# First attention, last six segments: the sum of the two gated terms moves from GpSimd into the turning on TensorE

## The chip, the cores and the metric

The kernel runs on one core of a Trainium2 chip. The metric is the device time of one launch in microseconds (us), lower is better. A profiled execution also has a span, from its first to its last recorded instruction. The engines are called TensorE (PE in the profile, its weight loads PEld), VectorE (DVE), ScalarE (ACT), GpSimd (POOL) and SyncE (SP).

## The reference, cut to what matters

The whole reference has two layers, each of an attention and a mixture of experts. The change lies in the first attention, which walks over segments of 64 tokens with a running memory `M` and normaliser `Z`:

```python
H, DK, DV, LSEG = (16, 64, 64, 64)          # B = 4 sequences of 512 tokens, D = 128
gate = sigmoid(betas)                        # one value per head and column v
def step(carry, seg):
    M, Z = carry
    q, k, v = ...                            # (B, H, 64, 64) each, of this segment
    scores = where(mask, -inf, q @ k.T / 8)
    att_dot = softmax(scores) @ v
    sq, sk = elu(q) + 1, elu(k) + 1
    att_mem = sq @ M / (sq @ Z.T)
    M_new, Z_new = M + sk.T @ v, Z + sk.sum(axis=-2)
    att = gate * att_mem + (1.0 - gate) * att_dot
    out = att.reshape(B, LSEG, H * DV) @ Wo
```

The sum in `att` is what the change is about: a gated memory term plus a gated softmax term, of which the product with `Wo` is then taken.

## The kernel before, in words

**Segments.** `attn0` walks over 32 segments `n` = 0 to 31, eight to a sequence. Each segment handles 64 tokens of 16 heads. A "segment" is one turn of the loop `for n in range(nseg)`; the order in which each engine gets its work is written out by hand there, and is kept (`pin`). The instructions of one segment are, in the order of the loop:

- `elu_exp(n + 1, 0)`: ScalarE, exp and relu of the next queries.
- `scores(n + 1)`: TensorE, 16 products `sc` (64x64), then VectorE the masked minimum `E` (line 686).
- `memory(n)`: TensorE, 16 products `mm`; VectorE a reciprocal `rm` (743) and the division `t` (744), which writes the tile `t1`; GpSimd multiplies it by the gate (763).
- `elu(n + 1, 0)`: VectorE, `elu` (709), which reads two tiles in SBUF.
- `turned(n - 2, n + 1)`: TensorE turns the finished attention of segment `n - 2` (eight transposes `tn<-ident,t`) and the elu keys of segment `n + 1` (eight transposes `tn<-ident,elu`), line 722, into one PSUM tile; ScalarE copies both out (`attT` in four pieces, `sk`).
- `update(n)`: TensorE, 16 products `mu`; VectorE adds them to the memory (`mz`, 778).
- `attend(n)`: TensorE, 16 products `dot`; VectorE a maximum and a reciprocal `rd` (797, 743), the division `t` (744, tile `t2`) and a maximum over sums (800); GpSimd multiplies by the other gate (801) and adds `t1` (802).
- `elu_exp(n + 2, 1)`, `scores_exp(n + 1)` on ScalarE, `elu(n + 2, 1)` on VectorE (709).

**Work between.** Up to segment 25 chunks of the q, k and v projections (`pp`, `pv`) stand in each segment as well; from segment 26 on there are none. Every fourth segment `output(h)` takes the 32 products `po` with `Wo`. In segment 31 and behind the loop the work of the next layer's experts (`ph`, `eo`) is mixed in, and `turned(30)`, `turned(31)` and `output(7)` come there.

**Buffers.** All of `sc`, `mm`, `tn`, `mu`, `dot`, `po`, `ph` take a tile of the same PSUM ring (`wide`), which has four buffers here: each takes the buffer of the fourth one before it, and waits until that one has been read. `t1` and `t2` have two buffers each, so segment `n` writes the tile of segment `n - 2`.

**Who waits for whom.** `mm` of segment `n` needs the memory that VectorE's `mz` of segment `n - 1` left. The turning of segment `n - 2` needs GpSimd's last write to `t2`.

Of the kernel before, what the change touches and what calls it, by code (L numbers as in the profile page):

```python
# [102 lines left out]
def bc(ap, axis, n):  # L103

    shape = list(ap.shape)
    return ap.unsqueeze(axis).to_broadcast(shape[:axis] + [n] + shape[axis:])


class Kernel:
# [257 lines left out]
    def wide(self, name):  # L367

        bufs = 4 if self.four else 3
        return self.banks.tile([P, 2, S], F32, name=name, tag="w", bufs=bufs)  # L370
# [228 lines left out]
    def attn0(self, xnT, g0, stack, between):  # L599
# [4 lines left out]
        nc, tc = self.nc, self.tc  # L604
        halves = [slice(0, 64), slice(64, 128)]
# [13 lines left out]
        for k in range(4):  # L619
            t = pool.tile([P, 4, 2, DK + 1], F32, name=f"vone{k}", bufs=1)  # L620
            nc.gpsimd.memset(t[:, :, :, DK : DK + 1], 1.0)
            vone.append(t)
        qkv, vd, attT, seg = {}, {}, {}, {}
# [45 lines left out]
        def blocks(n, w):  # L669
            s = n % 4  # L670
            return qkv[n // 4][w][:, s * 8 : s * 8 + 8, :]

        def scores(n):

            q, k = blocks(n, 0), blocks(n, 1)
            ps = wide(f"sc{n}")
            for hp in range(4):
                for p in range(2):
                    for a in range(2):
                        self.mm1(  # L680
                            ps[halves[a], p, hp * 64 : hp * 64 + 64],
                            lhsT=k[halves[p], 2 * hp + a, :], rhs=q[halves[p], 2 * hp + a, :],
                            start=True, stop=True,
                        )
            e = pool.tile([P, 2, 4, LSEG], F32, name=f"E{n}", tag="E")
            self.vec1(nc.vector.tensor_tensor(  # L686
                e, ps[:, :, 0:256].rearrange("p x (hp c) -> p x hp c", hp=4),
                bc(bc(self.cap, 1, 4), 1, 2), ALU.min,
            ))
            seg[n]["e"] = e  # L690
# [5 lines left out]
        def last(n):  # L696
            return n % 8 == 7
# [14 lines left out]
        def turned(att=None, own=None):  # L712

            ps = wide(f"tn{att}_{own}").rearrange("p x (w hp c) -> p x w hp c", w=2, hp=4)
            each = [(0, hp, x) for hp in range(4) for x in range(2) if att is not None]
            each += [(1, hp, x) for hp in range(4) for x in range(2) if own is not None]
            for w, hp, x in each:
                if w:
                    src = seg[own][1][halves[x], 2 * hp : 2 * hp + 2, :].rearrange("d a j -> d (a j)")
                else:  # L720
                    src = seg[att]["att"][halves[x], hp].rearrange("i p v -> i (p v)")
                self.pin(nc.tensor.transpose(ps[:, x, w, hp], src, self.ident[halves[x], halves[x]]))  # L722
            if att is not None:
                attended(att, ps[:, :, 0])
            if own is not None:
                t = seg[own]["sk"] = pool.tile([P, 4, 2, DK], F32, name=f"sk{own}", tag="sk")
                self.act1(t, ps[:, :, 1].rearrange("p x hp d -> p hp x d"), AF.Copy)

        def values(n):

            for p in range(2):
                src = vd[n // 4][p].rearrange("(s hp r) d -> s r hp d", s=4, hp=4)
                nc.sync.dma_start(out=vone[n % 4][:, :, p, 0:DK], in_=src[n % 4])

        def heads(ps):

            return ps[:, :, 0 : 4 * (DK + 1)].rearrange("p x (y v) -> p x y v", v=DK + 1)

        def over(t):
            return t.rearrange("p (x hp) y d -> p x (hp y) d", x=2)  # L740

        def divided(ps, t, r, sums):
            self.vec1(nc.vector.reciprocal(r, sums))
            self.vec1(nc.vector.tensor_tensor(t, heads(ps)[:, :, :, 0:DK], bc(r, 3, DK), ALU.mult))  # L744

        def memory(n):


            mz, sq = self.mz[(n % 8 + 1) % 2 + 1 if n % 8 else 0], seg[n][0]
            ps = wide(f"mm{n}")  # L750
            for hp in range(4):
                for p in range(2):
                    for a in range(2):
                        at = (2 * a + hp // 2) * (DK + 1)
                        self.mm1(
                            ps[halves[(a + hp) % 2], p, at : at + DK + 1],
                            lhsT=sq[halves[p], 2 * hp + a, :], rhs=mz[halves[p], hp, a, :],
                            start=True, stop=True,
                        )
            t = seg[n]["t1"] = pool.tile([P, 4, 2, DK], F32, name=f"t1{n}", tag="t1")  # L760
            r = pool.tile([P, 2, 4], F32, name=f"rm{n}", tag="rm")
            divided(ps, t.rearrange("p hp y d -> p y hp d"), r, heads(ps)[:, :, :, DK])
            nc.gpsimd.tensor_mul(t, t, self.gate)  # L763
# [16 lines left out]
        def attend(n):  # L780


            e, v = seg[n]["e"], vone[n % 4]
            ps = wide(f"dot{n}")
            for u in range(2):
                for p in range(2):
                    for hp in (2 * u, 2 * u + 1):
                        for a in range(2):
                            at = (2 * u + p) * (DK + 1)
                            self.mm1(  # L790
                                ps[halves[(a + hp) % 2], a, at : at + DK + 1],
                                lhsT=e[halves[a], p, hp, :], rhs=v[halves[a], hp, p, :],
                                start=True, stop=True,
                            )
            both = pool.tile([P, 2, 2, 4], F32, name=f"rd{n}", tag="rd")
            sums = both[:, 0]
            self.vec1(nc.vector.tensor_scalar_max(sums, heads(ps)[:, :, :, DK], SUM_MIN / 2))
            t = pool.tile([P, 4, 2, DK], F32, name=f"t2{n}", tag="t2")
            divided(ps, over(t), both[:, 1], sums)
            self.vec1(nc.vector.tensor_tensor(self.sums0, both, self.sums0, ALU.max))  # L800
            nc.gpsimd.tensor_mul(t, t, gate2)  # L801
            nc.gpsimd.tensor_add(t, t, seg[n]["t1"])  # L802
            seg[n]["att"] = t

        def attended(n, ps):

            if n % 4 == 0:

                attT[n // 4] = pool.tile([P, 16, 4, 32], F32, name=f"attT{n}", tag="attT")
            src = ps.rearrange("p h (a u) (t c) -> p c a u h t", a=2, c=16)  # L810
            dst = attT[n // 4][:, :, n % 4].rearrange("p c (u y t) -> p c u y t", u=2, y=4)
            for h in range(2):
                for a in range(2):
                    self.act1(dst[:, :, :, (a + h) % 2 * 2 + a], src[:, :, a, :, h], AF.Copy)
# [39 lines left out]
        for n in range(nseg):  # L854
            if n % 4 == 3:
                todo = project((n + 1) // 4 + 1)
            elif n == 0:
                todo = ahead
            each = 2 if n == 0 else 4 if n < 3 or n % 4 != 2 else 0
            nxt = n + 1 < nseg  # L860
            more = nxt and not last(n + 1)
            if n + 2 < nseg:
                values(n + 2)
            if nxt:
                elu_exp(n + 1, 0)
                scores(n + 1)
            memory(n)
            if nxt:
                elu(n + 1, 0)
            if n > 1 or more:  # L870
                turned(n - 2 if n > 1 else None, n + 1 if more else None)
            if not last(n):
                update(n)
            for f, *args in between.get(n - 0.5, []):
                f(*args)
            attend(n)
            ahead = n + 2 < nseg and not last(n + 2)
            if ahead:
                elu_exp(n + 2, 1)
            chunks, todo = todo[:each], todo[each:]  # L880
            for chunk in chunks[:1]:
                chunk()
            if nxt:
                scores_exp(n + 1)
            if ahead:
                elu(n + 2, 1)
            for chunk in chunks[1:]:
                chunk()
            for f, *args in between.get(n - 0.25, []):
                f(*args)  # L890
            if n % 4 == 2 and n > 4:
                output(n // 4 - 1)
            if not nxt:
                turned(n - 1)
            for f, *args in between.get(n, []):
                f(*args)
# [1680 lines left out]
```

## Time and profile before

| | |
|---|---|
| median of 3 runs | 686.84 us (685.57 to 686.98) |
| the profiled execution's own time | 687.07 us |
| its span | 685.3 us |
| granted TensorE clock, mean | 0.993 |
| busy: PE, DVE, ACT, POOL | 651.3, 502.8, 486.4, 347.0 us |
| segments 28 to 30 in the profile | about 280 to 296 us |

The profiled execution is 0.23 us above the median of the runs, and 1.77 us of it lie outside the span. TensorE is busy for 95% of the span, but busy time is a mean over stages with different limits: the chain of waits, followed back from the last instruction, changes the engine from stage to stage. The lines shown further on are in microseconds from the start of the span. In the timeline and in the groups a line gives the start, the busy time, the engine, the line of the kernel, the operation, and in brackets how long the engine sat idle before it and what ended that.

### The profile page before, as it was taken

The numbers are of one execution on the slowest core, as the hardware profiler recorded it, in microseconds if no ns is written. First come the engines' busy times: TensorE is split into PE (matmuls) and PEld (weight loads), VectorE is DVE, ScalarE is ACT, GpSimd is POOL, SyncE is SP. The second block draws the span as 40 slices with busy tenths as digits, with TensorE's granted clock in tenths as the row PEclk, the third lists the DMA queues.
The fourth block names the chain that finished last, engine by engine and source line by source line (L and its number), as shares of the span: only waits on it lengthen the run. The fifth ranks groups of instructions, "written<-read, shape, count | busy, mean of one in ns | idle before, by whom it ended". The sixth has DMA issues, their size and how long they took to land.

```text
span 685.3 us, 23640 instructions
## 1 busy us (share of the span) xinstructions
PE 651.3 (95%) x10051; PEld 405.7 (59%) x10051; DVE 502.8 (73%) x1084; ACT 486.4 (71%) x806; POOL 347.0 (51%) x383
## 2 busy tenths in 40 slices
PE   8999999999999899799999999999999999999994
PEld 4666667988978768677778863333444243422333
DVE  6876476676677968975378326879898999678874
ACT  4423478887877778653554479998998999899750
POOL 7490046777776666783753244213484752322170
PEclk9999999999999999999999999999999999999998
DMA  7750153233233222100035369777949684965300
GB/s 186 145 146 1 61 154 95 54 102 92 64 96 81 64 67 62 34 3 1 5 123 160 103 174 259 194 199 167 239 145 228 151 237 135 221 147 143 78 17 19
DMA packets 85488, 79.70 MB, mean 116 GB/s; under 512 B 42640, under 2 KB 74160, under 8 KB 82304
## 3 DMA queue, kind: packets, MB, share of 16 engines
q1 hardware_dynamic: 82544, 75.39, 41.8%
q0 software_dynamic: 2256, 2.47, 1.9%
q8 instruction: 81, 1.33, 0.8%
q10 hardware_dynamic: 576, 0.26, 0.1%
q14 instruction: 31, 0.25, 0.1%
HBM read 51.62 MB, written 26.21 MB: 114 GB/s over the span
## 4 chain that ended last, share of the span: by engine, by line
PE 71%; DVE 15%; ACT 10%; issue 2%; DMA 1%; POOL 1%; SPq 0%; DVEq 0%; ACTq 0%; POOLq 0%
PE acc L356 9%; ACT e L359 8%; PE eo L356 8%; PE pp L356 8%; PE ph L356 5%; PE po L356 5%; PE b L356 3%; PE pv L356 3%; PE pl L356 3%; PE s L356 3%; PE sc L356 2%; DVE elu L709 2%; PE den L356 2%; PE pg L356 2%; PE pu L356 2%
## 5 line engine op out<-in xcount | busy, mean ns | idle before, releaser
L359 ACT ACTIVATE e<-s 128x1024 f32<-128x1024 f32 x124 | 122.3, 1061 | 12.5 <-PE s L356 11.9
L356 PE MATMUL acc<-e,strip 128*32 128x512 f32 x1000 | 124.0, 598 | 0.9 <-DVE e L1971 0.9
L359 ACT ACTIVATE e<-e 128x1024 f32<-128x1024 f32 x104 | 107.8, 1100 | 0.0
L763 POOL TENSOR_TENSOR t<-t,gate 128x512 f32<-128x512 f32 x32 | 53.0, 1655 | 45.0 <-DVE t L744 45.0
L356 PEld LDWEIGHTS acc<-e,strip 128*32 128x32 f32 x1000 | 28.1, 109 | 70.2 <-issue 58.2
L801 POOL TENSOR_TENSOR t<-t,gate 128x512 f32<-128x512 f32 x32 | 50.1, 1565 | 29.5 <-DVE sums L800 26.0
L359 ACT ACTIVATE pj<-pp 128x512 f32<-128x512 f32 x64 | 38.6, 603 | 17.3 <-PE pp L356 15.6
L709 DVE SCALAR_TENSOR_TENSOR elu<-elu,up 128x512 f32<-128x512 f32 x60 | 46.9, 782 | 0.2
L359 ACT ACTIVATE h<-ph 128x1024 f32<-128x1024 f32 x20 | 20.5, 1025 | 35.9 <-PE ph L356 32.1
L686 DVE TENSOR_TENSOR E<-sc,cap 128x512 f32<-128x512 f32 x32 | 22.0, 687 | 32.1 <-PE sc L356 32.1
L356 PE MATMUL s<-q,k 64*128 64x512 bf16 x256 | 40.9, 382 | 3.6 <-ACT e L359 3.3
L356 PEld LDWEIGHTS <-k 64*128 64x128 bf16 x256 | 8.8, 94 | 59.8 <-issue 58.6
L802 POOL TENSOR_TENSOR t<-t,t 128x512 f32<-128x512 f32 x32 | 42.2, 1319 | 2.5
L356 PE MATMUL eo<-w_out,h 128*128 128x128 f32 x320 | 39.6, 278 | 0.0
L356 PEld LDWEIGHTS eo<-w_out,h 128*128 128x128 f32 x320 | 37.7, 192 | 3.2 <-issue 2.2
L359 ACT ACTIVATE elu<-pj 128x512 f32<-128x512 f32 x60 | 38.5, 642 | 0.1
L359 ACT ACTIVATE up<-pj 128x512 f32<-128x512 f32 x60 | 38.4, 639 | 0.0
L1752 POOL TENSOR_TENSOR pr<-pr,pr 128x512 f32<-128x512 f32 x14 | 22.5, 1630 | 30.3 <-DVE pr L1747 30.2
L359 ACT ACTIVATE attT<-tn 128x128 f32<-128x128 f32 x100 | 19.6, 282 | 20.5 <-PE tn L722 19.5
L1659 DVE TENSOR_TENSOR second<-second,first 128x1024 f32<-128x1024 f32 x16 | 27.0, 1694 | 8.3 <-DMA second<-qf 8.3
L356 PE MATMUL pp<-xnT,l0Wk 128*64 128x128 f32 x512 | 30.4, 274 | 2.5 <-issue 1.7
L356 PE MATMUL po<-l0wo,attT 64*128 64x128 f32 x512 | 30.7, 275 | 0.2 <-DVE t L744 0.2
(353 smaller groups left out, 1580.3 us busy)
## 6 DMA issues: line engine op xcount, KB each, us to landing
vd<-vt SPq DMA_DIRECT2D x32, 256.0 KB
vone<-vd SPq DMA_DIRECT2D x64, 128.0 KB
first<-qe SPq DMA_DIRECT2D x8, 1024.0 KB
second<-qf SPq DMA_DIRECT2D x16, 512.0 KB
third<-qf SPq DMA_DIRECT2D x32, 256.0 KB
qf<-qT SPq DMA_DIRECT2D x64, 64.0 KB
k<-kd SPq DMA_DIRECT2D x16, 256.0 KB
q<-qd SPq DMA_DIRECT2D x16, 256.0 KB
```

The source lines that it names most:

```text
L356: return self.pin(self.nc.tensor.matmul(*args, **kw))
L359: return self.pin(self.nc.scalar.activation(*args, **kw))
L686: self.vec1(nc.vector.tensor_tensor(e, ps[:, :, 0:256].rearrange("p x (hp c) -> p x hp c", hp=4), bc(bc(self.cap, 1, 4), 1, 2), ALU.min,))
L709: self.vec1(nc.vector.scalar_tensor_tensor(t, t, 1.0, up, ALU.min, ALU.add))
L763: nc.gpsimd.tensor_mul(t, t, self.gate)
L801: nc.gpsimd.tensor_mul(t, t, gate2)
L802: nc.gpsimd.tensor_add(t, t, seg[n]["t1"])
L1659: self.vec1(self.nc.vector.tensor_mul(t, t, self.first1[mm][:, two]))
L1752: self.nc.gpsimd.tensor_add(self.prod1[b, m], self.prod1[b, m], t)
```

## The change

For segments 26 to 31 (`n > 25`) `attend` no longer adds `t1` to `t2` on GpSimd; it hands both gated tiles on as a list. `turned` then takes plain products with the identity in place of transposes: for each of the eight blocks two products accumulate in PSUM, one with each term as the stationary operand, so that the sum is made while the block is turned. In segments 28 to 31 (`early`, `n > 27`) the turning of segment `n - 2` is placed ahead of `memory(n)`, and the own keys are turned behind it as before, in a PSUM tile of their own.

```diff
@@ turned
-                    src = seg[att]["att"][halves[x], hp].rearrange("i p v -> i (p v)")
+                    terms = [
+                        t[halves[x], hp].rearrange("i p v -> i (p v)") for t in seg[att]["att"]
+                    ]
+                    if len(terms) > 1:
+
+                        for k, term in enumerate(terms):
+                            self.mm1(
+                                ps[:, x, w, hp], lhsT=term, rhs=self.ident[halves[x], halves[x]],
+                                start=(k == 0), stop=(k == 1),
+                            )
+                        continue
+                    src = terms[0]
                 self.pin(nc.tensor.transpose(ps[:, x, w, hp], src, self.ident[halves[x], halves[x]]))
@@ attend
             nc.gpsimd.tensor_mul(t, t, gate2)
-            nc.gpsimd.tensor_add(t, t, seg[n]["t1"])
-            seg[n]["att"] = t
+            seg[n]["att"] = [t]
+            if n > 25:
+                seg[n]["att"].append(seg[n]["t1"])
+            else:
+                nc.gpsimd.tensor_add(t, t, seg[n]["t1"])
@@ the loop over segments
+            early = n > 27
+            if early:
+                turned(n - 2)
             memory(n)
             if nxt:
                 elu(n + 1, 0)
-            if n > 1 or more:
-                turned(n - 2 if n > 1 else None, n + 1 if more else None)
+            if more or n > 1 and not early:
+                turned(n - 2 if n > 1 and not early else None, n + 1 if more else None)
```

On the engines: GpSimd loses six instructions, TensorE gets 96 plain products in place of 48 transposes, and the number of VectorE and ScalarE instructions stays. The sequence of PSUM tiles in the ring changes in segments 28 to 31: segments 28 and 29 take one tile more, and in 28 to 31 the tile for the turning comes ahead of that for `mm`.

## The prediction

> **What bounds the kernel now.** I read the chain of waits first, since it says which engine sets the pace where the change lies, then the timeline of that stretch, then the busy time and clock by stretch. The chain:
>
> ```profile
> 285.62 0.69 DVE t L744
> 286.31 1.53 DVE elu L709
> 287.84 0.61 DVE mz L778
> ...
> 289.57 0.60 DVE elu L709
> 290.17 0.60 DVE E L686
> ...
> 291.68 1.54 DVE elu L709
> ...
> 295.76 0.70 DVE t L744
> 296.46 0.14 issue
> 296.60 3.84 PE po L356 x64
> 300.44 0.63 PE mm L356 x32
> 301.06 0.39 PE tn_None L722 x8
> 301.46 1.91 PE ph L356 x4
> 303.37 0.63 PE dot L356 x32
> 304.00 0.39 PE tn_None L722 x8
> ```
>
> From 281.2 to 296.5 every step is VectorE: a segment takes what VectorE's instructions take, 5.37 us (from `E` at 284.80 to `E` at 290.17). From 296.60 on every step is TensorE, without a gap, up to 404.6. So a saving counts where VectorE makes it (segments 28 to 30), and a cost counts where TensorE pays it (from `po` on). The two `elu` of 1.53 and 1.54 us stand out: the same instruction takes 0.60 at 289.57. The timeline shows why:
>
> ```profile
> 286.01 1.28 POOL L802 TENSOR_TENSOR t<-t,t 128x512 f32<-128x512 f32 x1
> 286.23 1.62 DVE L709 SCALAR_TENSOR_TENSOR elu<-elu,up 128x512 f32<-128x512 f32 x1
> ...
> 288.60 0.70 PE L356 MATMUL mm<-mz,elu 64*64 64x65 f32 x32 [1.45 <-DVE rd L797]
> ...
> 289.49 0.68 DVE L709 SCALAR_TENSOR_TENSOR elu<-elu,up 128x512 f32<-128x512 f32 x1
> 289.63 1.67 POOL L801 TENSOR_TENSOR t<-t,gate 128x512 f32<-128x512 f32 x1 [0.65 <-DVE sums L800]
> ```
>
> The slow `elu` began while GpSimd's addition ran, and ended at 287.85, 0.56 us after the addition's end (286.01 + 1.28 = 287.29). The quick one began ahead of GpSimd's multiply, and then the multiply was long (1.67, against 1.28 elsewhere). Whichever starts first makes the other wait. TensorE meanwhile idled 1.45 us ahead of `mm`. By stretch (columns: us and instructions of PE, PEld, DVE, ACT, POOL, then TensorE's clock, DMA share, GB/s):
>
> ```profile
> 281.19:286.56 5.37, 4.06 (x181) 3.46 (x185) 5.20 (x12) 3.14 (x10) 3.88 (x3) 1.00 0.24 52
> 286.56:291.93 5.37, 3.38 (x120) 2.95 (x123) 5.20 (x11) 3.66 (x11) 4.64 (x4) 0.85 0.01 3
> 291.93:296.60 4.67, 4.17 (x173) 3.69 (x165) 4.50 (x10) 3.12 (x9) 3.94 (x4) 0.81 0.02 4
> 296.60:306.10 9.50, 9.50 (x152) 6.95 (x153) 6.00 (x18) 3.77 (x10) 7.98 (x7) 1.00 0.02 4
> ```
>
> VectorE is full in the first three, TensorE in the last.
>
> **The change part by part.**
>
> *Six additions leave GpSimd* (26 to 31). Those of 27 and 28 (at 286.0 and 291.4) cover the two slow `elu`: without them each takes 0.60, so 0.93 + 0.94 = 1.87 us leave VectorE's chain. GpSimd's next multiply (763) doesn't take the addition's place: it waits for `t` (744), and `elu` follows `t` directly; in segment 27 `elu` began at 281.79 and took 0.68, the multiply at 281.95 took 1.66. The additions of 26 and 29 to 31 cover nothing on a path: beside 26 (277.6 to 278.9) VectorE runs small operations at their usual times, and from 29's on TensorE sets the end.
>
> *The shortened segment must still fit TensorE.* Without the stall VectorE needs 5.37 - 0.93 = 4.44 us. Start to start, TensorE needs about 0.58 for `sc` ahead of another shape, 0.39 for the own keys, 0.58 `mm`, 0.52 `mu`, 0.69 `dot`, plus the new turn.
>
> *The new turn.* Before: eight transposes, begun within 0.24 us, one from each half of the array's rows every 61 ns, 0.39 to the next instruction. After: 16 plain products. The trace has no plain product of this shape (64 rows, 128 columns, 64 moving); the nearest row is `po`, 64 rows, 128 columns, 128 moving: 32 products are 64 records and take 3.77 us to the next instruction, so a record for each half every 111 ns. With half the moving columns that is 56 ns, and no less than the 61 ns that the transposes show at the same 128 columns of weights. 16 products are 32 records, 16 per half: 16 x 0.06 = 0.96, and 0.11 for start and change of shape: 1.07 us. That is +0.68 per turn. From below: streaming alone, 0.90 (+0.5). From above: the halves don't overlap where four records in a row go to one half (`po` has two in a row), 32 x 0.06 = 1.92 (+1.6). I take 0.68, by the nearest row.
>
> A rule that speaks against the change: the Trainium skill, "TensorE: Matmul & The Clock Gate", section Terms, says that the transpose mode of trn2 is four times faster for FP32. By it each of two terms would cost four transposes' time, 8 x 0.24 = 1.95 us (+1.7 a turn, +5.1 in the tail below). The rows speak for less: at 64 moving columns the transposes run at 61 ns a pair, and two records of 56 to 61 ns are twice that for a term, not four times. I go by the rows and keep the rule at the far end of the range.
>
> *Turns of 26 to 28* lie in the VectorE-bound segments: 0.58 + 1.07 + 0.58 + 0.39 + 0.52 + 0.69 = 3.83 of 4.44 us. What hides them is the idle time ahead of `mm` (1.45 us before) and the place ahead of it; without that cover they cost +0.68 each. `mm` of 29 would come at about 288.2, its result is wanted at 289.8; `mm` of 30 at 292.6, wanted at 293.6. Queued behind the early turn are `mm`, `mu` and `dot`, for whose results VectorE would wait; the margin is 0.3 us in segment 30. The new turn waits for GpSimd's 801 of two segments ago, done over 1 us earlier. In the ring `mu` of 28 now waits for `E` of 29 (+0.2 us, inside its slack). ScalarE's copies come earlier, since the turn no longer shares a tile with the keys.
>
> *`po` starts without a wait for VectorE.* Before, it took the buffer of `mm` of 30 and began 0.14 behind VectorE's `t` (296.46). Now it takes that of the turn of 28, long copied out. `dot` of 30 still waits for `E` of 31 and starts at 295.69; the next shape follows `dot` by 0.66 (266.49 to 267.15), so 296.35: -0.25. Head in all: -1.87 - 0.25 = -2.12 us, `po` at about 294.5.
>
> *Turns of 29, 30, 31* lie in TensorE's own stretch: 3 x 0.68 = +2.04. The turn of 29 now follows `po` in the same shape, one change of shape less: -0.1 (four transposes a half need 0.24 of the 0.39). Nothing there was waiting for the additions: 802 of segment 31 ended at 307.96, its turn began at 309.74.
>
> *No DMA is added or moved*; SP's and POOL's queues of transfers stay.
>
> **Sum.** -2.12 + 2.04 - 0.1 = -0.2 us. The profiled execution took 687.07 (685.3 of span, 1.77 around), 0.23 above the median; it would take 686.9, and the median 686.84 becomes 686.6. Beyond 404 us ScalarE, VectorE and transfers take turns in the chain; I let the shift pass one to one.
>
> The runs before spread from 685.57 to 686.98, 0.2% or 1.4 us: less than that can't be told from no change.
>
> **Rivals.**
>
> *Slower: the two terms keep one half of the array waiting.* In the new order four records in a row go to the same 64 rows, then four to the others. If TensorE can't begin the other half past them, a turn costs 1.45 (three in four overlap in part) to 2.0. In the tail that is 3 x (1.06 to 1.6) = +3.2 to +4.8; in the head the turn of 28 delays `po` by 0.35 to 0.9. Sum: -1.8 + 3.2 to -1.2 + 4.8, so +1.4 to +3.6 us: 688.2 to 690.4. It decides from 0.75 us extra a turn on. For it: the rule above, and no row with four in a row. Against it: `mm`, whose 32 records cover four quarters and still begin four every 59 ns, so that three records are passed over.
>
> *Faster: the tail pays less than the head gains.* If the turn costs +0.2 to +0.3 only, because the following product of another shape begins inside it, the tail is +0.8 and the sum -1.4; with the shift growing in the DMA-fed stretch behind 404 us, where transfers are at 75 to 80%, up to -2.2: 684.6 to 685.4. For it: each short burst in the chain carries 0.15 us of change of shape, which a longer one spreads. Against it: 61 ns a pair is already shown.
>
> *The change doesn't do what it says in the head:* some other GpSimd instruction meets `elu`. The multiply 801 of 29 must end before `elu` of 31 at 294.5; it ends about 0.1 ahead. Then at most 0.9 comes back, but behind 294.5 TensorE leads, so nothing.
>
> **How the numbers follow.** Wash 0.48 (likeliest; its own range 685.6 to 687.8), slower 0.25, faster 0.27. The wash spills a little over the bound on either side, 0.04 each: faster 0.31, same 0.40, slower 0.29. Range for 8 in 10: 684.9 to 689.0.
>
> **What would show it.** Both long `elu` at about 0.60; segments 28 and 29 at 4.44 us; `po` at 294.5; the turn in the chain at about 1.07 instead of 0.39, thrice behind `po`; `eo` first at 305.3 instead of 306.1, the next turn taking the rest back. Turns over 1.4 make the slower rival right, turns under 0.7 the faster one. The loss of clock in the second and third stretch (0.15 x 5.37 + 0.19 x 4.67 = 1.7 us of TensorE's time) now hides behind VectorE; it should go, as TensorE idles less. If it stays, the shortened segments have some 0.6 us each to spare for it, and 0.5 to 1 us would come onto the path.

## The result, and the profile after

The changed kernel takes 690.4 us in the median of 6 runs (689.15 to 694.49), the kernel before on the same chip 687.14 (685.57 to 687.70): a ratio of 1.0058, 95% interval 1.0039 to 1.0077, slower by 3.3 us in the medians and 4.0 by the ratio. The profiled execution of after is the longest of its six, 694.49 us with a span of 692.7, against 687.07 and 685.3; so its account below comes to 7.4 us, more than the median's. "Head" is the stretch from the fourth last `E` to the last but one `po`, "tail" that from there to the last `po`. A "record" is one entry of the trace; a plain FP32 product leaves two records on TensorE, each with a weight load of its own. Its weight columns are those of the operand that is loaded into the array, its moving columns those that are then streamed through it.

The chain of waits of after, in the same stretch (start and length in us, what):

```profile
282.65 1.98 PE tn_None L356 x32
284.63 0.63 PE mm L356 x32
...
287.69 1.98 PE tn_None L356 x32
...
292.35 1.03 PE tn_None L356 x13
293.38 0.60 issue
293.98 1.33 PE tn_None L356 x18
295.31 1.05 PE mm L356 x32
296.36 0.87 PE mu L356 x32
297.23 0.87 PE dot L356 x32
298.10 4.09 PE po L356 x64
302.18 1.84 PE tn_None L356 x32
304.02 0.62 PE mm L356 x32
...
307.19 1.98 PE tn_None L356 x32
```

Before, the chain ran over VectorE up to 296.5; now it is TensorE's from 282 on. Each turn with two terms costs 1.98 us to the next instruction (1.84 right behind `po`) where 0.39 stood before. Two further things are new here: an "issue" of 0.60 us inside a turn, which the profile explains by nothing, and, later, `mm`, `mu` and `dot` at 1.05, 0.87 and 0.87 us instead of the 0.62, 0.47 and 0.47 of the chain of `few_dear` below. The timeline says that the aim was reached all the same:

```profile
286.25 0.68 DVE L709 SCALAR_TENSOR_TENSOR elu<-elu,up 128x512 f32<-128x512 f32 x1
...
291.38 0.68 DVE L709 SCALAR_TENSOR_TENSOR elu<-elu,up 128x512 f32<-128x512 f32 x1
...
296.42 0.21 DVE L754 RECIPROCAL rm<-mm 128x8 f32<-128x8 f32 x1 [1.96 <-PE mm L356]
```

Both long `elu` are gone (1.62 before). But VectorE now sits idle 1.96 us for TensorE's `mm`. By stretch, with TensorE's granted clock in the third column from the end:

```profile
284.65:289.25 4.60, 4.39 (x165) 4.10 (x166) 4.36 (x12) 3.98 (x10) 3.34 (x3) 1.00 0.03 5
289.25:293.78 4.53, 4.13 (x157) 3.71 (x156) 3.75 (x10) 2.94 (x8) 2.80 (x2) 1.00 0.02 4
293.78:298.03 4.25, 4.05 (x116) 3.86 (x115) 2.19 (x7) 1.30 (x5) 1.73 (x2) 0.68 0.01 4
```

VectorE is busy 4.36, 3.75 and 2.19 us of these, TensorE 4.39, 4.13 and 4.05. The half clock lasts 3.413 us in both kernels; before it stood at 290.30, where VectorE hid it, now at 295.31, on the path.

Cut at four common points, the profiles differ so (the points are the fourth last `E`, at 280.28 in before, the two last `po`, and the sixth last and the last `eo`, near 375 and 402; the stretch from `po` to the sixth last `eo` is 61.79 or 61.80 in every kernel of this study and left out):

| us | `E` to `po` | `po` to `po` | `eo` to `eo` | `eo` to end |
|---|---|---|---|---|
| before | 16.31 | 17.23 | 26.90 | 282.75 |
| after | 17.81 | 22.17 | 26.90 | 283.79 |

The head, which should have become 2.1 us shorter, is 1.50 longer; the tail is 4.94 longer instead of 2.0; 1.04 comes at the end, where TensorE waits 1.29 us ahead of a product `b` (in the chain behind a transfer, `second<-qf`, of 14.84 us).

### The profile page after: what moved, and what is told of

Its sections match the earlier page's. It is cut to its first block, busy times and chain, and to the rows that moved or that the text cites. A ratio compares the mean times of both kernels' runs of the same rounds, so it can differ in the third digit from the quotient of the medians.

```text
span 692.7 us, 23924 instructions
## 1 busy us (share of the span) xinstructions
PE 661.2 (95%) x10195; PEld 415.8 (60%) x10195; DVE 501.1 (72%) x1084; ACT 487.1 (70%) x806; POOL 339.8 (49%) x377
## 4 chain that ended last, share of the span: by engine, by line
PE 70%; DVE 16%; ACT 7%; DMA 3%; issue 2%; POOL 1%; SPq 0%; DVEq 0%; ACTq 0%; POOLq 0%
PE eo L356 8%; PE pp L356 8%; PE acc L356 7%; ACT e L359 6%; PE ph L356 5%; PE po L356 5%; PE pv L356 3%; PE b L356 3%; PE s L356 2%; PE sc L356 2%; DMA second<-qf 2%; PE pl L356 2%; PE mu L356 2%; PE dot L356 2%; PE pg L356 2%
## 5 line engine op out<-in xcount | busy, mean ns | idle before, releaser
L817 POOL TENSOR_TENSOR t<-t,t 128x512 f32<-128x512 f32 x26 | 34.0, 1308 | 2.0
L356 PEld LDWEIGHTS po<-l0wo,attT 64*128 64x128 f32 x512 | 29.5, 189 | 2.1 <-PE pgr L356 0.8
```

What stands on the lines that cost most here:

```text
L356: return self.pin(self.nc.tensor.matmul(*args, **kw))
```

## The experiments

The theory after this profile: a plain product of this shape costs by its 128 weight columns and not by its 64 moving ones, so the turn is 1.98 us; that fills the tail one to one and makes TensorE the bound of the head. Rivals: the order of the records keeps one half of the array waiting; and, for the head, something else than the turn's time. The kernels ran in four groups, each on one chip with its own runs of before; the table at the end of this section has them in this order with all ratios.

**The head alone, no additions at all, and the turn in two other forms.** `head_only` uses two terms only for segments 26 to 28:

```diff
-            if n > 25:
+            if 25 < n < 29:
...
-            early = n > 27
+            early = 27 < n < 31
```

> Two terms on TensorE for segments 26 to 28 alone (turned in 28 to 30, ahead of mm); segments 29 to 31 keep GpSimd's addition and transposes. Theory (the loss is the three dear turns behind po, 1.59 us each, 4.7 us in all; the head itself gains): faster than before by 1 to 1.8 us, po beginning at 295 to 295.6 instead of 296.6, nothing lost behind it. Rival (the head loses as well: TensorE is the bound of segments 28 to 30 with turns of 1.98 us, stalls of its instructions and the half clock): po at 297 to 298, slower than before by 0.5 to 1.5 us.

`no_add` is before without the six additions (it leaves the memory term out of the attention of 26 to 31):

```diff
-            nc.gpsimd.tensor_add(t, t, seg[n]["t1"])
+            if n < 26:
+                nc.gpsimd.tensor_add(t, t, seg[n]["t1"])
```

> The kernel before without the six additions of segments 26 to 31 and with nothing in their place (the memory term is left out of the attention there). Theory (the additions of 27 and 28 hold up VectorE's elu, and nothing else comes in): both elu at 0.60 instead of 1.53, po 1.9 us earlier, 1.9 us faster than before. Rival (another GpSimd instruction or TensorE takes the place of the stall): 0 to 0.9 us faster, a long elu or an idle VectorE in segments 28 to 30.

`alternate` is after with the two terms as the outer loop and the halves of the array in turn inside; `quarters` also splits each product in two of 64 weight columns (64 records a turn instead of 32). Both in short:

```diff
+                for hp in range(4):
+                    for k, t in enumerate(seg[att]["att"]):
+                        for x in range(2):
+                            for y in range(2):        # quarters only
+                                self.mm1(ps[halves[y], x, 0, hp], lhsT=t[halves[x], hp, y], ...)
```

> The change with the same 16 products a turn, but the two halves of the array's rows taken in turn: term outside, half inside, so that two records in a row go to one half instead of four. Theory A (order: a half can't load its next weights under its own product when four records in a row are its own): the turn falls from 1.98 to about 1.1 us, the tail from +4.7 to +2.1, the kernel within 1 us of before. Theory B (price: a plain FP32 product with 128 weight columns takes 111 ns a half and record whatever the moving columns and the order): the turn stays at 1.98, the kernel 3 to 4 us slower than before, as the change.

> As alternate, but each product split into two with 64 weight columns each, so that the four quarters of the array work side by side: 32 products a turn, 64 records. Theory B (weight columns are the price; mm, with 64 weight columns, shows four records every 59 ns): 16 x 59 ns and 0.15, so 1.1 us a turn, the tail +2.1, the kernel within 1 us of before. Theory A (order alone): as cheap as alternate, both at 1.1. If the number of records is the price, the turn is 1.98 or more and the kernel slower than the change.

Measured: 1.0022, 0.9952, 1.0057 and 1.0066. The order of the records changes nothing: in the chain of `alternate` the turn still reads

```profile
306.29 1.93 PE tn_None L356 x32
```

and in after's trace two records, one for each half, already begin within some 15 ns of each other, then the next two 112 ns later. So the halves do overlap, and each takes a record every 112 ns. With 64 weight columns, in the head and in the tail of `quarters`:

```profile
289.04 0.35 PE tn_None L356 x24
289.39 1.71 issue
291.10 0.81 PE tn_None L356 x40
...
308.51 0.93 PE tn_None L356 x64
```

The turn is 0.93 us (1.09 in the two others of the tail), for the same 64 moving columns and twice the records: at this shape the price goes by weight columns. Rows of before that the prediction did not use say the same, and where it ends (the first line from the chain, the others from the timeline):

```profile
247.75 1.88 PE lp L356 x16
...
247.68 1.95 PE L356 MATMUL lp<-wg,gT 32*128 32x8 f32 x16
...
260.33 3.47 PEld L356 LDWEIGHTS pp<-xnT,l0Wk 128*64 128x64 f32 x64
260.33 3.71 PE L356 MATMUL pp<-xnT,l0Wk 128*64 128x128 f32 x64
```

`lp` has 128 weight columns and only 8 moving ones, and its records begin 112 ns apart; `pp` has 64 weight columns and 128 moving ones, and in each column half of the array a record begins every 109 ns. With 59 ns for `mm` (64 and 65), 112 for `po` (128 and 128) and 429 for `ph` (128 and 512), the greater of the two numbers of columns sets the time of a plain FP32 record in all these rows.

The tail of `quarters` is then +2.01 us (`po` to `po` 19.24), about the +2.04 that I had predicted for the change. But its head is the longest of all, `E` to `po` 19.12, with "issue" in the middle of groups: 0.92, 1.71, 1.33 and 1.86 us. So its whole time misses both expectations that gave it a cheap turn. The head alone loses 1.5 us, in its profile 0.61 up to `po` and 0.85 in `po` and behind, although `no_add` gains 3.3 (1.29 up to `po`, where 1.9 was expected, the rest behind the last `eo`). So a second cause may sit in the head.

**Time or number of instructions?** TensorE's instructions come in packets of a DMA queue of their own; the page of after:

```profile
PE 661.2 (95%) x10195; PEld 415.8 (60%) x10195; DVE 501.1 (72%) x1084; ACT 487.1 (70%) x806; POOL 339.8 (49%) x377
...
q8 instruction: 82, 1.34, 0.9%
```

20,390 records and 252 semaphore and other instructions over 82 packets are 252 a packet, and `quarters`, with some 380 records more, has 84 packets. A turn of two terms has 48 records more than one of transposes. To tell the number from the time, three kernels leave out the additions of 26 to 28 (and so the memory term there) and have the early place of the turn: `early_no_add` is the control; `many_cheap` makes each of the eight transposes four times; `few_dear` puts two products in front, which the transposes overwrite. `tail_only` has two terms for 29 to 31 alone.

```diff
 many_cheap
+                for _ in range(4 if not w and 25 < att < 29 else 1):
+                    self.pin(nc.tensor.transpose(...))
 few_dear
+                for x, end in enumerate((512, 340)):
+                    self.mm1(ps[:, x]...[:, 0:end], lhsT=self.ident, rhs=self.wqkv[2][:, 0:end], ...)
 tail_only
-            if n > 25:
+            if n > 28:
-            early = n > 27
+            early = n > 30
```

> Control for the head: the memory term of segments 26 to 28 is left out of the attention (no addition on GpSimd), the turns of 26 to 28 stay eight transposes each and stand ahead of memory, as in the change; segments 29 to 31 as before. If the new place of the turn costs nothing: as without any of the six additions, 683.3 to 684.3 us, both elu 0.68 us, TensorE waiting for instructions at most 1 us in segments 28 to 30. Rival, the new place itself costs: 684.8 us or more.

> The control, with each of the eight transposes of the turns of 26 to 28 made four times: 48 more TensorE instructions a turn, as many as the change adds, but only 24 x 30 ns = 0.73 us more of work instead of 1.59. Theory of the instruction supply (256 instructions come at least some 3.8 us apart, so 336 a segment take 5.0 us and not 4.4): 1 to 2 us above the control, with 1 to 2 us of idle TensorE inside groups. Rival, only the time of the records counts (0.6 us a segment is free): within 0.5 us of the control.

> The control, with two products of 512 and 340 columns in front of each of the turns of 26 to 28, overwritten by the transposes: about 1.6 us more of TensorE a turn, as much as the change adds, but only 8 instructions instead of 48. Theory of the supply: TensorE needs 4.7 us a segment instead of 4.4, so 0.3 to 1 us above the control. Rival, the time of the turn alone made the head lose: as the head alone, about 688 us, 4 us above the control.

> The two terms only for segments 29 to 31, whose turns lie behind po; GpSimd adds for 26 to 28 as before. By the measured price of a turn (1.98 instead of 0.39): 3 x 1.59 = 4.8 us slower than before, 691.4 us, with 22 us between the two last po instead of 17.2. If the end behind 404 us takes part of it back: 1 to 3 us slower.

Measured: 0.9961, 1.0015, 0.9985, 1.0101. `E` to `po` is 14.32 us in the control, 15.14 with the dear turn (+0.8), 15.62 with the many cheap ones (+1.3). The control's head is 1.99 us shorter than before's 16.31, close to the 2.12 predicted for the head; with the dear turns it is still 1.17 shorter. The chains of `few_dear` and of `many_cheap`, the turn of 28:

```profile
291.17 1.63 PE tn_None L356 x4
292.80 0.39 PE tn_None L728 x8
293.19 0.62 PE mm L356 x32
293.81 0.47 PE mu L356 x32
294.28 0.47 PE dot L356 x32
```

```profile
290.24 0.64 PE tn_None L723 x13
290.88 1.00 issue
291.88 0.84 PE tn_None L723 x18
292.72 0.62 PE mm L356 x32
```

A turn of 2.02 us in few instructions runs without a stop and with most of its cost hidden; one of 1.2 us in many stops TensorE for 1.00 us. Both expectations of the supply hold for this stretch. In whole times both miss them: they lose 2.3 and 3.2 us against the control, since on this chip another stretch differs too (last experiment).

Where TensorE stops says more. Count all its records in the trace from the start (products, weight loads and semaphore instructions); between 280 and 300 us the stops of over 0.15 us that have no other engine's work to wait for end at four numbers (idle time in us; what is blank showed none):

```
record       11969   12225   12481   12737
after         0.21            0.60
no_add        0.55            0.67
alternate             0.47    0.72    0.19
quarters      0.92    1.71    1.33    1.86
many_cheap            0.73    1.00    0.42
head_only                     0.81
tail_only     0.30
half_adds             0.59    0.74
merged                0.20    1.03
merged_half                   0.75
after_again                   0.34
head_again                    0.27    0.19
tail_third    0.82
```

The steps are 256, about a packet's worth, and the operation there differs: a turn in after, `mu` in `no_add`, `dot` in `merged`. Each idle time ends 2.2 to 2.9 us after a packet of that queue has begun (after: packet at 291.36, go on at 293.98; `merged`: 293.58 and 295.76). The Trainium skill, "Runtime: NRT & Kernel Launch", section "Instruction fetch mechanics", has the blocks of 256 instructions too, but calls the cost of crossing into the next mostly hidden. None shows in segments 28 to 30 of before, where VectorE sets a pace of 5.37 us; in a dense stretch it is up to 1.9 us here, and the measurement decides. It could have been seen in before itself, on its chain, ahead of the stretch that the prediction read:

```profile
258.12 0.45 PE dot L356 x27
258.57 1.50 issue
260.07 0.34 PE dot L356 x5
```

This stop is at record 10433, six times 256 ahead of 11969. Of the six stops of over 0.15 us in the whole trace of before that wait for no other engine, five lie on these marks (0.46, 0.18, 0.23, 1.28 and 1.50 us).

In `quarters`, where stops follow each other, packets come 3.7 to 4.2 us apart.

**Other ways to the same saving.** `half_adds` leaves TensorE's program as before and cuts the additions of 27 and 28 in two; `merged` is before with one transpose of 128 rows in place of two of 64 in the turnings of segments 26 to 30 (16 records fewer in most); `merged_half` does both.

```diff
 half_adds, in the loop
             memory(n)
+            if n in (28, 29):
+                added(n - 1, 0)          # half of the columns
...
             attend(n)
+            if n in (28, 29):
+                added(n - 1, 1)
 merged, in turned
+                        self.pin(nc.tensor.transpose(
+                            ps[:, w, hp * P : hp * P + P], src.rearrange("d a j -> d (a j)"), self.ident
+                        ))
```

> TensorE's part as before; GpSimd still adds for all six segments, but the additions of 27 and 28 are cut into two halves of about 0.65 us, one behind the next memory term's multiply (763), one behind the next softmax term's multiply (801), where VectorE is not in elu by the timeline. Theory (the two long elu are what the additions cost): each elu about 0.7 to 0.9 instead of 1.62, po some 1 to 1.5 us earlier, 1 to 2 us faster than before. Rival (GpSimd is full then, so the stall only moves to another elu): within 0.5 us of before.

> Before, with the merged transposes alone. VectorE sets the pace there and TensorE hardly waits for instructions: within 0.5 us of before. If fewer instructions alone are worth something: 1 us faster.

> As half_adds, and in segments 26 to 30 one transpose of 128 rows takes the place of the two of 64 rows (8 instead of 16 in a turning, 16 TensorE instructions fewer a segment, some 0.2 us more of TensorE a turn). Theory (the instruction supply held back half_adds, whose TensorE idled 0.58 and 0.74 us at the 256-instruction marks): those two stalls go or shrink below 0.4 us together, po comes 0.5 to 1 us earlier than in half_adds, 1 to 2 us faster than before. Rival (VectorE and GpSimd hold it back): as half_adds, within 0.5 us of before.

Measured: 0.9992 (interval 0.9977 to 1.0008), 1.0025 and 1.0018: no gain. GpSimd's order is not kept in this kernel, and both halves ran behind each other where the whole had been; `elu` slipped in after the first half:

```profile
285.34 1.87 POOL L809 TENSOR_TENSOR t<-t,t 128x256 f32<-128x256 f32 x2
...
285.55 1.07 DVE L709 SCALAR_TENSOR_TENSOR elu<-elu,up 128x512 f32<-128x512 f32 x1
```

That takes 1.1 us out of two `elu` and `po` comes only 0.42 earlier (15.89): TensorE stops at 12225 and 12481 instead. So the step from VectorE's saving to the time fails even where no turn is dearer. My expectation that fewer instructions would mend it was wrong: `merged_half` has `po` later still (16.18), and in `merged`, which is 1.5 us slower than before in the medians, the stop is at the very same record, now in the `dot` right before `po`:

```profile
294.34 0.39 PE dot L356 x22
294.73 1.03 issue
295.76 0.35 PE dot L356 x8
```

Its packet began 113 records ahead of the mark; in before on the same chip the packet for that mark began 208 ahead, and there is no stop. What decides when a packet is asked for, I could not settle; the number of instructions alone is not it.

**Do head and tail add up?** Whole, head and tail on one chip, then the tail beside a profile of before:

> The whole change, on one chip with its two parts. If the parts add up: the sum of what the head alone and the tail alone lose, 5 to 8 us. If they don't: 3 to 4 us as in the first comparison, and the tail alone loses less than it did on the other chip or the head gains when the tail follows.

> The two terms only for 26 to 28, as in the earlier run of the head alone: 1 to 2 us slower than before if that was the head and not the chip.

> The two terms only for 29 to 31, on the chip of the whole change: 4.8 us slower by the price of three turns; 7 us if what it lost beyond that on the other chip comes with the kernel.

> Before itself, for its profile on this chip. If the idle TensorE in pl near 380 us comes with the chip: it is there too, and the stretch from eo at about 375 to eo at about 402 takes 30 us or more instead of 26.9. If it comes with the changes: 26.9 us.

> The tail alone beside a profile of before from the same chip. By the turns alone 4.6 to 4.8 us slower; 7 us again if more comes with it, and then the profile shows which stretch is longer than in before of this chip.

| kernel (a group: one chip) | ratio to before, 95% | `E` to `po` | `po` to `po` | `eo` to `eo` | `eo` to end |
|---|---|---|---|---|---|
| head_only | 1.0022, 1.0010 to 1.0033 | 16.92 | 18.08 | 26.90 | 283.67 |
| no_add | 0.9952, 0.9936 to 0.9969 | 15.02 | 17.23 | 26.90 | 280.76 |
| alternate | 1.0057, 1.0041 to 1.0072 | 16.67 | 22.11 | 26.90 | 282.99 |
| quarters | 1.0066, 1.0051 to 1.0082 | 19.12 | 19.24 | 26.90 | 281.68 |
| early_no_add | 0.9961, 0.9943 to 0.9979 | 14.32 | 17.23 | 29.90 | 282.83 |
| many_cheap | 1.0015, 0.9994 to 1.0036 | 15.62 | 17.93 | 32.56 | 283.29 |
| few_dear | 0.9985, 0.9967 to 1.0003 | 15.14 | 17.23 | 32.70 | 282.89 |
| tail_only | 1.0101, 1.0076 to 1.0125 | 16.32 | 21.82 | 32.25 | 286.90 |
| half_adds | 0.9992, 0.9977 to 1.0008 | 15.89 | 17.23 | 30.26 | 285.67 |
| after_again | 1.0073, 1.0051 to 1.0096 | 15.94 | 22.04 | 33.56 | 283.19 |
| head_again | 1.0035, 1.0017 to 1.0052 | 15.66 | 17.69 | 34.17 | 287.62 |
| tail_again | 1.0104, 1.0078 to 1.0131 | 16.30 | 21.82 | 33.50 | 285.06 |
| before_again | (one run, 685.58 us) | 16.31 | 17.23 | 26.90 | 282.80 |
| merged | 1.0025, 1.0011 to 1.0038 | 17.28 | 17.23 | 26.90 | 283.50 |
| merged_half | 1.0018, 1.0001 to 1.0036 | 16.18 | 17.23 | 26.90 | 282.81 |
| tail_third | 1.0084, 1.0059 to 1.0109 | 16.31 | 21.82 | 26.90 | 284.33 |

They don't add up: on one chip the head costs 0.35%, the tail 1.04%, both together 0.73%. The head alone is 0.61 us longer up to `po` than before in `head_only`, with a stop of 0.81 us and half clock behind it, and 0.65 shorter in `head_again`, with stops of 0.27 and 0.19 us and full clock. `po` to `po` is steady: +4.59 for the tail alone on three chips, three turns of +1.59, less 0.18, mostly because the first follows `po` in the same shape. The rest lies later and differs from chip to chip. In the second and third group TensorE idles in `pl` near 380 us, in the chain of `tail_again`:

```profile
384.50 0.77 PE pl L356 x32
385.27 1.16 issue
386.43 0.30 PE pl L356 x2
```

These stops are not at multiples of 256 records. The half clock follows them in both tail kernels, in `after_again`, `head_again`, `many_cheap` and `few_dear`, and not in `half_adds` (TensorE's instructions as before) and `early_no_add`; that is what makes 32 to 34 us of 30. In the first and fourth group the stretch is 26.90 in all profiles, `before_again` among them; its chip turned out to be one without these stops, so it can't tell whether before has them on the other two. The medians of before there, 691.7 and 692.0 us against 685.7 to 687.1 elsewhere, suggest it. On the fourth chip the tail still loses 5.9 us (1.0084): 4.6 in the turns, and in its profile 1.53 more behind the last `eo`, where TensorE waits ahead of a product `b` near 445 as in after. Why the whole loses less than the tail is left open: the two profiles differ by 2 us behind the last `eo`, which a single execution each can't explain.

## Why the prediction was wrong

- **VectorE's stall: right.** The two additions covered the two long `elu`; both fell to 0.68 us.
- **The price of the turn: the step that failed.** The sum took 1.07 us from `po`'s row, halving its 111 ns because half as many columns move. Measured 1.98: a record with 128 weight columns takes a half 112 ns for 64 moving columns as for 128. The term "half the moving columns, 56 ns" was wrong, and the floor of 61 ns came from transposes, which run far quicker than plain products at the same columns. `po`, with 128 columns on both sides, can't tell which side sets the price; `lp` (128 weight columns, 8 moving ones, 112 ns) could have, in the trace of before. The Trainium skill's rule that I set at the far end (transposes four times faster, 1.95 us a turn) had the size right, and `quarters` shows the dimension: 64 weight columns, 0.93 to 1.09 us.
- **The tail: mechanism right, size off by that term.** +4.94 instead of +2.04 and -0.1: three turns of 1.84, 1.98 and 1.98 for three of 0.39 are +4.63, and `po` in half clock is +0.32.
- **"The shortened segment must still fit TensorE": failed.** 3.83 of 4.44 us becomes 4.74 with the real turn. The segments took 4.60 and 4.53, and `po` came at 298.03 instead of 294.5. Of these 3.5 us, 0.91 in each of three turns is the price, less the slack that the segments had; 0.81 are stops (0.21 and 0.60), by the marks for instructions, which no step of mine had; 1.23 is half clock in `mm`, `mu` and `dot`. Without these two the dear turns take back only part of the head's gain: `few_dear`, with turns of 2.02 us, no stop and full clock, reaches `po` 1.17 us earlier than before.
- **The half clock: half right.** I wrote that it should go, and that 0.5 to 1 us would come onto the path if it stayed. It moved, and took 1.55 with `po`'s share. In `after_again` it isn't in the head at all, and `E` to `po` is 15.94, 0.4 shorter than before: the head's result differs by 1.9 us between these two executions of the same kernel.
- **Rivals.** The slower one had size (1.45 to 2.0 a turn, 688.2 to 690.4 us) and side right and the mechanism wrong: `alternate` refutes the waiting half. The faster one needed turns under 0.7 us, and none was under 1.84; no other GpSimd instruction met an `elu`.
- **A shift passes one to one: right up to 402 us** on the quick chips, where every stretch from `po` to the last `eo` is the same; behind it 1 us more came.

## What to carry to other kernels

Price a plain FP32 product by the greater of its weight columns and its moving columns, a transpose by a row of its own kind, and never take one's duration for the other's. If the nearest row has both numbers equal, look for one that has not before halving its time. If a sum is moved to TensorE, count weight loads and instructions, not flops. When VectorE or GpSimd is relieved, work out what TensorE then needs in time and in instructions a microsecond, and look in the trace for stops that nothing explains and for the number of records between them: the segments of before, 288 records in 5.37 us, showed none, and most kernels with segments of 3.9 to 4.7 us did (the control and `few_dear` did not). A wait that is hidden by a slower engine (late instructions, half clock) can become part of the price of making that engine faster.

## What the runs showed of the hardware that was not expected

- A plain FP32 record took 112 ns with 128 weight columns, whether 8, 64 or 128 columns moved, and 109 ns with 64 weight columns and 128 moving ones.
- TensorE stops at fixed records 256 apart whatever stands there, in the dense stretch for 0.2 to 1.9 us, and goes on 2.2 to 2.9 us after a packet of the instruction queue began. That these stops are late instructions is inferred from the steps and the packets; the profile only says "issue".
- Half clock of 3.413 us began 1.3 us after the stop of 0.60 us ended in `after` and 1.9 us after that of 0.81 us in `head_only`, but not after those of 0.67 us in `no_add`, 1.03 in `merged` or 1.86 in `quarters`; before has it at 290.30 without such a stop. That the stops bring it is not shown.
- The same kernel before took 685.7 to 692.0 us on the chips used, and TensorE's idle time in `pl` appears in every profile of two of them and in none of the others.
